# Forming spectral matrices in the first stage, loading layer 1's weights early, and moving the last image's put-back beside the long scan

## The chip, the cores and the metric

The kernel runs on one core of one Trainium2 chip. A core has five engines that matter here: TensorE (PE in the profile), VectorE (DVE), ScalarE (ACT), GpSimd (POOL) and SyncE (SP), which in this kernel does nothing but issue every DMA, in program order. The metric is the time of the whole program on the device, in microseconds (us). All arithmetic is in 32-bit floating point.

## What is computed

The input is four images of 128 channels and 64 x 64 pixels, 4096 tokens each. Two layers follow one another; cut to what matters:

```
# layer 0, per image
score  = gated two-convolution score of every 4x4 patch        # orders the 256 patches
x1n    = layernorm(x_reordered + pe)
xz     = x1n @ in_proj.T                                       # then conv1d, silu, dt, B, C
h      = dA_t * h + dB_t * x_t         # 16 states, 256 channels, 4096 steps
out_m  = (ys + D * xc) * silu(z) @ out_proj.T
x      = x + put_back(out_m)           # patches return to their places in the image

# layer 1, tokens of every image
state  = exp(delta A) * state + delta B x                      # 256 states, 256 channels
y      = state . C                     # then * silu(z) @ W_out, added to the tokens
t      = t + y
t      = t + sum over 4 branches of weight_i *
             ( sum_k conv(phi_k, t) @ (sigma_k**0.25 * M_plus[i, k])  # first 1/1, 1/2, 1/4, 1/8
             + the same with M_minus on sign-alternated tokens + a 3-tap term with M_u[i] )
```

The four branches act on the first 4096, 2048, 1024 and 512 tokens. Since they differ only in where they stop, their matrices can be added up beforehand: for every filter k and every range of tokens there is one summed matrix for M_plus and one for M_minus, and from these the sum P and the difference Q that the kernel multiplies with. These are the "spectral matrices". They depend on weights alone.

## The kernel before

The program is four stages in a row, each of which is a Python function that emits instructions.

`layer0_front` handles one image after another: statistics of the image, two 3 x 3 depthwise convolutions (four taps on TensorE, five on VectorE as `scalar_tensor_tensor` into the tile `sum`, line 105), Gelu on ScalarE (lines 187 and 209), the patch scores, the order of the patches as a permutation matrix (`perm_t`), and the ordered tokens (`xn`, written to DRAM as `xnt`). The order of instructions in this stage is chosen by the framework's own scheduler.

`layer0_scan` is scheduled by hand. It walks through 32 units of 512 tokens with a scan of 16 states on VectorE (line 506), and hides the projection of the next unit and the output of the last one beside it. Its function `put_back` takes the finished tokens of an image (`om`), multiplies them with `perm_t` on TensorE, adds the image (`xs`, line 440) and writes `x2`. For the last image this comes after the last scan.

`spectral_weights` loads M_plus and M_minus for each of the 16 filters (`raw`), sums the branches in `branch_sums` (a chain of `scalar_tensor_tensor` on VectorE), multiplies with sigma and writes P and Q to DRAM (`pqd`), and the summed M_u (`mud`).

`layer1` is scheduled by hand as well. It loads its weights, projects the first 512 tokens, and then runs 8192 steps: 32 parts (image, 512 tokens) of 256 states. One step of the loop `for k in range(-8, steps)` issues, for different states ahead of the current one:

- `fetch` (line 1084): a DMA that spreads two rows of delta over all partitions (`dlb`, four buffers), 8 steps ahead;
- `carry` (lines 1092 and 1093): two GpSimd instructions for 32 states that bring the last state of the part before into the first column, 6 steps ahead, in 28 of the 32 parts;
- `spread` (line 1098): the GpSimd product `v` for two states (three buffers), 4 steps ahead, and a small ScalarE copy (line 1102) that fills in the first column;
- `lift` (line 1107): two exponentials on ScalarE into `da`, which lies in PSUM in two buffers, 1 step ahead;
- `scan` (line 1110): the scan of one state on VectorE into `s`.

Every eight steps `contract` multiplies `s` with C on TensorE, copies the result with ScalarE into `ye` (one buffer, line 1133), writes it to DRAM (`yd`) and reads it back turned (`yt`). `beside` is a generator that hides two kinds of work in small pieces: `output` of the part before and `project` of the part after. A piece that says "free" moves one step, a piece that says "mm" or "post" moves at the seventh and eighth of each eight steps. Both call `normalise`, in which GpSimd forms `rs` and `ms` (lines 772 and 773) and ScalarE then uses them (line 777). `products` is a second generator: the convolutions of the spectral filters (`conv`, line 1058) and the products with P and Q (`fin`, line 1002) on TensorE, with `load` fetching `pq` (five buffers) and `strip` two items ahead. It goes by a credit per step, and what is left when the steps are over forms the tail.

Of the kernel before, what the change touches and what calls it, by code (L numbers as in the profile page):

```python
# [15 lines left out]
NB = 4  # L16
# [4 lines left out]


@with_exitstack
def layer0_front(ctx: ExitStack, tc, ident, half, w, x, xnt, perm_t):

# [84 lines left out]
    def by_patch(t, oy):  # L110

        return t.rearrange("c (py px oy ox) -> c oy py px ox", px=16, oy=4, ox=4)[:, oy]

    for b in range(NB):

        xs = xp.tile([128, L], F32, tag="xs", name="xs")
        nc.sync.dma_start(xs, x[b])
        st = sm.tile([128, 8, 6], F32, tag="st", name="st")
        for q in range(8):
            nc.vector.bn_stats(st[:, q, :], xs[:, bass.ts(q, 512)])  # L120
# [157 lines left out]


@with_exitstack  # L280
def layer0_scan(ctx: ExitStack, tc, ident, w, x, xnt, perm_t, x2):

# [250 lines left out]
    def gated(j):  # L533
        n, i, g = place(j)
        if i == 0:
            ygs[n] = big.tile([128, 2, PJ], F32, tag="yg", name="yg")
        cols = bass.ts(i, SUB)
        nc.vector.tensor_tensor(ygs[n][:, :, cols], y.pop((n, i)), ready[n][0][:, 2:4, cols], ALU.mult)
        if i == PJ // SUB - 1:
            b, unit = units[n]  # L540
            if unit == 0:
                oms[b] = big.tile([128, 2, 16, 128], F32, tag="om", name="om")
            behind.append(output(b, unit, ygs.pop(n), oms[b]))
            if unit == L // PJ - 1:
                behind.append(put_back(b, oms[b]))

    class Work:
        def __init__(self, pieces):
# [54 lines left out]
    gated(steps - 1)  # L603
    while holder or rear and rear.kind or behind:
        beside(steps)


TS = 512
# [4 lines left out]
NK = 16  # L613


@with_exitstack
def spectral_weights(ctx: ExitStack, tc, sigma, m_u, m_plus, m_minus, log_w, gumbel, pqd, mud):
# [39 lines left out]
    nc.vector.memset(quarter, 0.25)  # L657
    nc.gpsimd.tensor_tensor(sig, sig, quarter, ALU.pow)

    def branch_sums(dst, src):  # L660

        nc.vector.tensor_scalar(dst[:, 3], src[:, 0], wt[:, 0:1], None, ALU.mult)
        for i in range(1, 4):
            nc.vector.scalar_tensor_tensor(
                dst[:, 3 - i], src[:, i], wt[:, i : i + 1], dst[:, 4 - i], ALU.mult, ALU.add
            )

    mu = mp.tile([128, 4, 3, 128], F32, name="mu", bufs=1)
# [3 lines left out]
    branch_sums(mue, mu)  # L672
    nc.sync.dma_start(mud, mue)
    for k in range(NK):
        raw = mp.tile([128, 2, 4, 128], F32, tag="raw", name="raw")
        nc.sync.dma_start(raw[:, 0], m_plus[:, k].rearrange("i d e -> d i e"))
        nc.sync.dma_start(raw[:, 1], m_minus[:, k].rearrange("i d e -> d i e"))
        sums = mp.tile([128, 2, 4, 128], F32, tag="sums", name="sums")
        for side in range(2):
            branch_sums(sums[:, side], raw[:, side])  # L680
        nc.vector.tensor_scalar(sums, sums, sig[:, k : k + 1], None, ALU.mult)
        pq = mp.tile([128, 2, 4, 128], F32, tag="pq", name="pq")
        nc.vector.tensor_tensor(pq[:, 0], sums[:, 0], sums[:, 1], ALU.add)
        nc.vector.tensor_tensor(pq[:, 1], sums[:, 0], sums[:, 1], ALU.subtract)
        for side in range(2):
            nc.sync.dma_start(pqd[k, side], pq[:, side])


@with_exitstack
def layer1(ctx: ExitStack, tc, ident, half, w_in, w_delta, w_b, w_c, w_out, a_t, phi, pqd, mud, x2, x3, out):  # L690

# [27 lines left out]
    win = wp.tile([128, 512], F32, name="win")  # L719
    nc.sync.dma_start(win, w_in)  # L720
    wbd = wp.tile([128, 2, 512], F32, name="wbd")
    wc = wp.tile([128, 2, 256], F32, name="wc")
    for t, s in ((wbd[:, :, 0:256], w_b), (wbd[:, :, 256:512], w_delta), (wc, w_c)):
        nc.sync.dma_start(t, s.rearrange("(k p) n -> p k n", p=128))
    wo = wp.tile([128, 2, 128], F32, name="wo")
    nc.sync.dma_start(wo, w_out.rearrange("(k p) n -> p k n", p=128))
    at = wp.tile([128, 2, 256], F32, name="at")
    nc.sync.dma_start(at, a_t.rearrange("(k p) d -> p k d", p=128))
# [28 lines left out]
    def normalise(t):  # L757
# [13 lines left out]
        rs = sm.tile([128, NT], F32, tag="rs", name="rs")  # L771
        nc.gpsimd.tensor_tensor(rs, ve, half[:, :NT], ALU.pow)
        nc.gpsimd.tensor_tensor(ms, ms, rs, ALU.mult)
        yield "free"
        yield "free"
        for i in range(NT):
            nc.scalar.activation(  # L777
                t[:, i, :], t[:, i, :], AF.Identity, bias=ms[:, i : i + 1], scale=rs[:, i : i + 1]
# [12 lines left out]
    def project(b, ch, into):  # L791
# [73 lines left out]
                nc.vector.tensor_tensor(af[:, h, bass.ts(j, 128)], ps[:, 0:128], at[:, h, bass.ts(j, 128)], ALU.mult)  # L865
        yield "free"
        nc.scalar.activation(af, af, AF.Exp)

    tokens = {}

# [90 lines left out]
    def load(i):  # L961
# [125 lines left out]
    def carry(ch, d, ready):  # L1087

        af, vf = ready[4:]
        cols = bass.ds(d, 32)  # L1090
        if ch:
            nc.gpsimd.tensor_tensor(af[:, :, cols], af[:, :, cols], last[:, :, cols], ALU.mult)
            nc.gpsimd.tensor_tensor(vf[:, :, cols], vf[:, :, cols], af[:, :, cols], ALU.add)
# [21 lines left out]
    def contract(s, c, g, keep):  # L1115
# [13 lines left out]
                    )  # L1129

        def put(j):
            ye = wk.tile([128, 2, 32, GD], F32, tag="ye", name="ye", bufs=1)
            nc.scalar.copy(ye, yp[j].rearrange("p i d t -> p i t d"))  # L1133
            nc.sync.dma_start(yd[0:128, 2 * j : 2 * j + 2], ye)

# [56 lines left out]
    for k in range(-8, steps):  # L1192
# [62 lines left out]
def conv_attn_hybrid(ctx: ExitStack, tc, w, out):  # L1255
# [9 lines left out]
    x = w["x"]  # L1265
    with tc.tile_pool(name="ordered", bufs=1) as pool:
        xnt = dram.tile([NB, 128, 3 + L], F32, name="xnt")
        perm_t = pool.tile([128, NB, 2, 256], F32, name="perm_t")
        layer0_front(tc, ident, half, w, x, xnt, perm_t)
        layer0_scan(tc, ident, w, x, xnt, perm_t, x2)  # L1270
    pqd = dram.tile([NK, 2, 128, 4, 128], F32, name="pqd")
    mud = dram.tile([128, 4, 3, 128], F32, name="mud")
    spectral_weights(
        tc, w["sigma"], w["M_u"], w["M_phi_plus"], w["M_phi_minus"], w["log_weights"], w["gumbel"], pqd, mud
    )
    layer1(
        tc, ident, half, w["W_in"], w["W_delta"], w["W_B"], w["W_C"], w["W_out"], w["A"], w["phi"], pqd, mud,
        x2, x3, out,
    )


# ---- launch: one core; the host only lays the inputs out
# [45 lines left out]
```

## Time and profile before

| | us |
|---|---|
| time, median of 3 runs | 21922.89 |
| lowest and highest run | 21910.68, 21937.1 |
| span of the profiled execution | 21920.9 |
| busy, DVE | 20589.4 (94%) |
| busy, POOL | 20181.2 (92%) |
| busy, PE | 17505.8 (80%) |
| busy, ACT | 15831.5 (72%) |

The stages can be told apart in the timeline. The first stage ends with the last write of `xnt` at 569 us. The 16-state scan lasts from 642 us to 2753 us; the put-back of the last image follows until 2798 us, the spectral matrices until 2880 us, and the start of layer 1 until the first scan of 256 states at 2940 us. The 8192 steps last until 21566 us, and the tail until 21921 us. So a share of the whole span is an average over stages of which one, the 256-state loop, is 85%. Busy time counts an engine's own instructions; a row of the page gives how often a kind of instruction ran, the mean length of one, and the idle time of the engine just ahead of it.

### The profile page before, as it was taken

The numbers are of one execution on the slowest core, as the hardware profiler recorded it, in microseconds if no ns is written. First come the engines' busy times: TensorE is split into PE (matmuls) and PEld (weight loads), VectorE is DVE, ScalarE is ACT, GpSimd is POOL, SyncE is SP. The second block draws the span as 40 slices with busy tenths as digits, with TensorE's granted clock in tenths as the row PEclk, the third lists the DMA queues.
The fourth block names the chain that finished last, engine by engine and source line by source line (L and its number), as shares of the span: only waits on it lengthen the run. The fifth ranks groups of instructions, "written<-read, shape, count | busy, mean of one in ns | idle before, by whom it ended". The sixth has DMA issues, their size and how long they took to land.

```text
span 21920.9 us, 291965 instructions
## 1 busy us (share of the span) xinstructions
PE 17505.8 (80%) x98516; PEld 7675.8 (35%) x98516; DVE 20589.4 (94%) x11984; ACT 15831.5 (72%) x29148; POOL 20181.2 (92%) x5932
## 2 busy tenths in 40 slices
PE   7788844565858888877768888869498899999999
PEld 4344311232323333333323333324143344334344
DVE  6788979999999999999999999999999999999993
ACT  3677757777777777777777777777777777777773
POOL 0677769999999999999999999999999999999993
PEclk8999966676979999988979999979699999999999
DMA  0455544555756776666656777757477777777775
GB/s 31 123 139 140 140 143 150 168 181 159 215 171 217 219 222 216 219 206 193 200 185 215 221 218 219 220 180 228 154 232 217 225 232 233 231 231 230 229 227 152
DMA packets 2399968, 4238.08 MB, mean 193 GB/s; under 512 B 778200, under 2 KB 1235968, under 8 KB 2395136
## 3 DMA queue, kind: packets, MB, share of 16 engines
q1 hardware_dynamic: 2398464, 4219.40, 62.8%
q8 instruction: 776, 12.71, 0.2%
q14 instruction: 728, 5.96, 0.1%
HBM read 3600.52 MB, written 617.88 MB: 192 GB/s over the span
## 4 chain that ended last, share of the span: by engine, by line
DVE 50%; POOL 17%; PE 11%; ACT 9%; issue 7%; DMA 3%; SPq 0%; DVEq 0%; POOLq 0%; ACTq 0%
DVE s L1110 43%; POOL v L1098 17%; ACT da L1107 6%; PE conv L1058 5%; DVE states L506 3%; DMA yd<-ye 2%; PE yp L1127 2%; DVE p L510 1%; PE fin L1002 1%; ACT f L498 1%; PE y L522 1%; PE mm L415 1%; ACT t L777 0%; ACT ye L1133 0%; ACT xz L362 0%
## 5 line engine op out<-in xcount | busy, mean ns | idle before, releaser
L1098 POOL TENSOR_TENSOR v<-u,dlb 128x2044 f32<-128x2044 f32 x4096 | 18342.6, 4524 | 108.9 <-DMA dlb<-delta 89.9
L1110 DVE TENSOR_TENSOR_SCAN s<-da,v 128x1024 f32<-128x1024 f32 x8192 | 18055.4, 2269 | 384.0 <-ACT da L1107 309.2
L1107 ACT ACTIVATE da<-dlb,at 128x511 f32<-128x511 f32 x16384 | 11299.4, 690 | 2064.5 <-DVE s L1110 1599.6
L1058 PE MATMUL conv<-strip,tok 128*128 128x512 f32 (+3 forms) x20480 | 8653.9, 552 | 6.7 <-DMA strip<-in_phi 6.6
L1127 PE MATMUL yp<-s,c 128*32 128x256 f32 x65536 | 5011.0, 437 | 2958.7 <-DVE s L1110 1611.9
L1058 PEld LDWEIGHTS conv<-strip,tok 128*128 128x128 f32 x20480 | 3696.9, 193 | 4126.2 <-issue 3743.4
L1127 PEld LDWEIGHTS yp<-s,c 128*32 128x32 f32 x65536 | 1990.3, 121 | 6745.9 <-issue 1835.0
L1102 ACT COPY v<-vf 128x4 f32<-128x4 f32 x4096 | 813.3, 199 | 2262.8 <-DVE s L1110 2139.2
L484 POOL TENSOR_TENSOR v<-dx,bcb 128x1024 f32<-128x1024 f32 x512 | 1207.3, 2358 | 434.5 <-DVE states L506 427.6
L1002 PE MATMUL fin<-conved,pq 128*128 128x512 f32 (+1 forms) x3200 | 1423.6, 540 | 13.2 <-ACT conved L1069 4.4
L506 DVE TENSOR_TENSOR_SCAN states<-f,v 128x1024 f32<-128x1024 f32 x512 | 1175.9, 2297 | 173.1 <-ACT f L498 124.3
L1133 ACT COPY ye<-yp 128x512 f32<-128x512 f32 x2048 | 1185.9, 579 | 136.2 <-DMA yd<-ye 123.4
L498 ACT ACTIVATE f<-dt,an 128x255 f32<-128x255 f32 x2048 | 973.5, 476 | 419.0 <-DVE states L506 368.2
L522 PE MATMUL y<-p,ident 128*128 128x512 f32 x2048 | 1008.7, 622 | 147.3 <-DVE p L510 142.2
L1069 ACT COPY conved<-conv 128x512 f32<-128x512 f32 x1344 | 778.1, 579 | 340.4 <-PE conv L1058 339.4
L510 DVE TENSOR_TENSOR p<-states,bcb 128x1024 f32<-128x1024 f32 x512 | 627.0, 1225 | 39.3 <-DVE states L506 0.9
L1002 PEld LDWEIGHTS fin<-conved,pq 128*128 128x128 f32 x3200 | 533.3, 195 | 227.1 <-issue 165.8
L522 PEld LDWEIGHTS y<-p,ident 128*128 128x128 f32 x2048 | 370.2, 196 | 680.5 <-issue 355.7
L415 PE MATMUL mm<-ow,yg 128*32 128x128 f32 x2048 | 282.1, 297 | 106.8 <-ACT om L419 105.3
L415 PEld LDWEIGHTS mm<-ow,yg 128*32 128x32 f32 x2048 | 236.2, 139 | 213.0 <-ACT om L419 128.4
L136 POOL TENSOR_TENSOR rs<-sq,half 128x1 f32<-128x1 f32 x4 | 2.2, 559 | 329.6 <-DVE sq L134 329.6
L1018 DVE TENSOR_TENSOR xo<-xo,fin 128x512 f32<-128x512 f32 x32 | 21.3, 667 | 300.8 <-PE fin L1010 300.8
(239 smaller groups left out, 6143.4 us busy)
## 6 DMA issues: line engine op xcount, KB each, us to landing
dlb<-delta SPq DMA_DIRECT2D x4096, 512.0 KB, 4.1
strip<-in_phi SPq DMA_DIRECT2D x1536, 448.0 KB, 4.8
yd<-ye SPq DMA_DIRECT2D x2048, 256.0 KB, 4.0
bcb<-bcd SPq DMA_DIRECT2D x1024, 256.0 KB, 4.2
strip<-in_phi SPq DMA_DIRECT2D x1024, 256.0 KB, 4.3
pq<-pqd SPq DMA_DIRECT2D x1088, 64.0 KB, 3.9
yt<-yd SPq DMA_DIRECT2D x4096, 4.0 KB, 3.4
pq<-pqd SPq DMA_DIRECT2D x256, 128.0 KB, 4.1
```

Of the source, the lines that this page charges most:

```text
L484: nc.gpsimd.tensor_tensor(v, ready[n][2][:, :, bass.ts(i, SUB)].unsqueeze(1).broadcast_to((128, 2, 2, SUB)), bc[:, 0].unsqueeze(2).broadca ...
L498: nc.scalar.activation(factors[j % 2][:, a, k, 1:], ready[n][1][:, k, SUB * i + 1 : SUB * i + SUB], AF.Exp, scale=an[:, k, 2 * g + a : 2 * ...
L506: nc.vector.tensor_tensor_scan(states.rearrange(flat), factors[j % 2].rearrange(flat), v.rearrange(flat), 0.0, ALU.mult, ALU.add)
L510: nc.vector.tensor_tensor(p, states, bc[:, 1].unsqueeze(2).broadcast_to((128, 2, 2, SUB)), ALU.mult)
L522: nc.tensor.matmul(t.rearrange("p k t -> p (k t)"), ident, p[:, a].rearrange("p k t -> p (k t)"), start=g == 0 and a == 0, stop=False, ski ...
L1002: nc.tensor.matmul(fin[:, bass.ds(c0, w)], pq[:, n, :], u[:, bass.ds(c0, w)], start=begin and n == 0, stop=end and not partly, skip_group_ ...
L1058: nc.tensor.matmul(ps[:, skip:], tok[:, 1 - r if side else r, j, :], strip[:, bass.ds(c0 - lo, TS - skip)], start=src == sources[0] and j ...
L1098: nc.gpsimd.tensor_tensor(v[:, :, :, 1:], ready[0][:, :, 1:].unsqueeze(1).broadcast_to((128, VD, 2, TS - 1)), dl[:, :, 1:].unsqueeze(2).br ...
L1107: nc.scalar.activation(da[:, h, 1:], dl[:, d % VD, 1:], AF.Exp, scale=at[:, h, d : d + 1])
L1110: nc.vector.tensor_tensor_scan(s[:, d % GD].rearrange("p h t -> p (h t)"), da.rearrange("p h t -> p (h t)"), v[:, d % VD].rearrange("p h t ...
L1127: nc.tensor.matmul(yp[i // 2][bass.ts(q, 32), i % 2], c[:, h, t], s[:, :, h, t], start=h == 0, stop=h == 1)
L1133: nc.scalar.copy(ye, yp[j].rearrange("p i d t -> p i t d"))
```

## The change

Five things are done in one edit.

1. `spectral_weights` becomes a generator that `layer0_front` calls: a few filters at a time are emitted from the second image on, and the framework's scheduler places the instructions. The work moves to other engines: `branch_sums` scales on ScalarE (four copies of 256 values per filter, with weight times sigma in `both`) and adds on GpSimd (three additions of 256 values per filter, on both sides at once), and P and Q (512 values each) are formed on GpSimd.
2. `layer1_weights` loads the weights of layer 1 between the first two stages, into tiles that live as long as the program.
3. The put-back of the last image leaves `layer0_scan`. Its tokens and its permutation go to DRAM (`omd`, `permd`), and a new `put_back` in `layer1` does it in eight pieces beside the first part, in the place where the other parts have `output`.
4. `carry` takes 128 states at a time, 10 steps ahead.
5. `ye` gets two buffers, `pq` four in place of five, and `normalise` waits three steps more between GpSimd and ScalarE.

```
-def layer0_front(ctx: ExitStack, tc, ident, half, w, x, xnt, perm_t):
+def layer0_front(ctx: ExitStack, tc, ident, half, w, x, xnt, perm_t, pqd, mud):
...
+    matrices = spectral_weights(
+        ctx, tc, w["sigma"], w["M_u"], w["M_phi_plus"], w["M_phi_minus"], w["log_weights"], w["gumbel"], pqd, mud
+    )
     for b in range(NB):
...
         nc.sync.dma_start(xs, x[b])
+        for _ in range(6 if b else 0):
+            next(matrices, None)
...
             if unit == L // PJ - 1:
-                behind.append(put_back(b, oms[b]))
+                if b < NB - 1:
+                    behind.append(put_back(b, oms[b]))
...
+    for h in range(2):
+        nc.sync.dma_start(omd[h], oms[NB - 1][:, h])
...
-    def branch_sums(dst, src):
-
-        nc.vector.tensor_scalar(dst[:, 3], src[:, 0], wt[:, 0:1], None, ALU.mult)
+    both = cp.tile([128, 4, NK], F32, name="both")
+    for i in range(4):
+        nc.vector.tensor_scalar(both[:, i, :], sig, wt[:, i : i + 1], None, ALU.mult)
+
+    def branch_sums(dst, src, weight):
+
+        for i in range(4):
+            nc.scalar.activation(dst(3 - i), src(i), AF.Copy, scale=weight(i))
         for i in range(1, 4):
-            nc.vector.scalar_tensor_tensor(
-                dst[:, 3 - i], src[:, i], wt[:, i : i + 1], dst[:, 4 - i], ALU.mult, ALU.add
-            )
+            nc.gpsimd.tensor_tensor(dst(3 - i), dst(3 - i), dst(4 - i), ALU.add)
...
-        for side in range(2):
-            branch_sums(sums[:, side], raw[:, side])
-        nc.vector.tensor_scalar(sums, sums, sig[:, k : k + 1], None, ALU.mult)
+        branch_sums(lambda r: sums[:, :, r], lambda i: raw[:, :, i], lambda i: both[:, i, k : k + 1])
...
-        nc.vector.tensor_tensor(pq[:, 0], sums[:, 0], sums[:, 1], ALU.add)
-        nc.vector.tensor_tensor(pq[:, 1], sums[:, 0], sums[:, 1], ALU.subtract)
+        nc.gpsimd.tensor_tensor(pq[:, 0], sums[:, 0], sums[:, 1], ALU.add)
+        nc.gpsimd.tensor_tensor(pq[:, 1], sums[:, 0], sums[:, 1], ALU.subtract)
...
-        yield "free"
-        yield "free"
+        for _ in range(5):
+            yield "free"
...
+    def put_back():
+
+        b = NB - 1
+        image = lambda t, h, oy: t[b].rearrange("c (y oy x) -> c y oy x", oy=4, x=64)[:, bass.ts(h, 8), oy, :]
+        for h in range(2):
+            for oy in range(4):
+                om = wide().rearrange("p r (i c) -> p r i c", i=4)
+                for r in range(2):
+                    nc.sync.dma_start(om[:, r], omd[r][:, bass.ts(oy, 4)])
+                perm = sm.tile([128, 2, 128], F32, tag="mu", name="perm", bufs=1)
+                nc.sync.dma_start(perm, permd[:, :, bass.ts(h, 128)])
+                xs = small().rearrange("c (py x) -> c py x", x=64)
+                nc.sync.dma_start(xs, image(x, h, oy))
+                yield "mm"
+                ps = middle()
+                for ox in range(4):
+                    for r in range(2):
+                        nc.tensor.matmul(
+                            ps[:, bass.ts(ox, 128)], om[:, r, ox, :], perm[:, r, :], start=r == 0, stop=r == 1
+                        )
+                yield "post"
+                dst = xs.rearrange("c py (px ox) -> c py px ox", ox=4)
+                nc.vector.tensor_tensor(
+                    dst, dst, ps.rearrange("c (ox py px) -> c py px ox", ox=4, px=16), ALU.add
+                )
+                nc.sync.dma_start(image(x2, h, oy), xs)
...
-            pq = sp.tile([128, 2, 128], F32, tag="pq", name="pq", bufs=5)
+            pq = sp.tile([128, 2, 128], F32, tag="pq", name="pq", bufs=4)
...
-        cols = bass.ds(d, 32)
+        cols = bass.ds(d, 128)
...
-            ye = wk.tile([128, 2, 32, GD], F32, tag="ye", name="ye", bufs=1)
+            ye = wk.tile([128, 2, 32, GD], F32, tag="ye", name="ye")
...
             yield from output(*parts[n - 1], done.pop(n - 1), ready.pop(n - 1)[2])
+        else:
+            yield from put_back()
...
-        j = k + 6
-        if 0 <= j < steps and j % 32 == 0:
+        j = k + 10
+        if 0 <= j < steps and j % 128 == 0:
...
+        weights = layer1_weights(nc, const, *(w[k] for k in ("W_in", "W_delta", "W_B", "W_C", "W_out", "A")))
+        omd = dram.tile([2, 128, 16, 128], F32, name="omd")
+        permd = dram.tile([128, 2, 256], F32, name="permd")
+        nc.sync.dma_start(permd, perm_t[:, NB - 1])
```

More of the change, by code (lines that the diff above doesn't have):

```diff
@@ L280, in layer0_scan @@
 @with_exitstack
-def layer0_scan(ctx: ExitStack, tc, ident, w, x, xnt, perm_t, x2):
+def layer0_scan(ctx: ExitStack, tc, ident, w, x, xnt, perm_t, x2, omd):
     nc = tc.nc
@@ L613, with spectral_weights @@
 NK = 16
-@with_exitstack
-def spectral_weights(ctx: ExitStack, tc, sigma, m_u, m_plus, m_minus, log_w, gumbel, pqd, mud):
+def spectral_weights(ctx, tc, sigma, m_u, m_plus, m_minus, log_w, gumbel, pqd, mud):
     nc = tc.nc
@@ L671, in spectral_weights @@
     mue = mp.tile([128, 4, 3, 128], F32, name="mue", bufs=1)
-    branch_sums(mue, mu)
+    branch_sums(lambda r: mue[:, r], lambda i: mu[:, i], lambda i: wt[:, i : i + 1])
     nc.sync.dma_start(mud, mue)
+    yield
     for k in range(NK):
@@ L678, in spectral_weights, with layer1_weights, layer1 @@
         sums = mp.tile([128, 2, 4, 128], F32, tag="sums", name="sums")
-        for side in range(2):
-            branch_sums(sums[:, side], raw[:, side])
-        nc.vector.tensor_scalar(sums, sums, sig[:, k : k + 1], None, ALU.mult)
+        branch_sums(lambda r: sums[:, :, r], lambda i: raw[:, :, i], lambda i: both[:, i, k : k + 1])
         pq = mp.tile([128, 2, 4, 128], F32, tag="pq", name="pq")
-        nc.vector.tensor_tensor(pq[:, 0], sums[:, 0], sums[:, 1], ALU.add)
-        nc.vector.tensor_tensor(pq[:, 1], sums[:, 0], sums[:, 1], ALU.subtract)
+        nc.gpsimd.tensor_tensor(pq[:, 0], sums[:, 0], sums[:, 1], ALU.add)
+        nc.gpsimd.tensor_tensor(pq[:, 1], sums[:, 0], sums[:, 1], ALU.subtract)
         for side in range(2):
             nc.sync.dma_start(pqd[k, side], pq[:, side])
+        yield
+def layer1_weights(nc, pool, w_in, w_delta, w_b, w_c, w_out, a_t):
+    win = pool.tile([128, 512], F32, name="win")
+    nc.sync.dma_start(win, w_in)
+    wbd = pool.tile([128, 2, 512], F32, name="wbd")
+    wc = pool.tile([128, 2, 256], F32, name="wc")
+    for t, s in ((wbd[:, :, 0:256], w_b), (wbd[:, :, 256:512], w_delta), (wc, w_c)):
+        nc.sync.dma_start(t, s.rearrange("(k p) n -> p k n", p=128))
+    wo = pool.tile([128, 2, 128], F32, name="wo")
+    nc.sync.dma_start(wo, w_out.rearrange("(k p) n -> p k n", p=128))
+    at = pool.tile([128, 2, 256], F32, name="at")
+    nc.sync.dma_start(at, a_t.rearrange("(k p) d -> p k d", p=128))
+    return win, wbd, wc, wo, at
 @with_exitstack
-def layer1(ctx: ExitStack, tc, ident, half, w_in, w_delta, w_b, w_c, w_out, a_t, phi, pqd, mud, x2, x3, out):
+def layer1(ctx: ExitStack, tc, ident, half, weights, phi, pqd, mud, x, omd, permd, x2, x3, out):
     nc = tc.nc
@@ L717, in layer1 @@
     pf = ctx.enter_context(tc.tile_pool(name="s_pf", bufs=1, space=PSUM))
[L719 to L728, printed above, removed]
+    win, wbd, wc, wo, at = weights
     ones = wp.tile([128, 128], F32, name="ones")
@@ L1190, in fetch_y @@
                 take(done[m])
-    for k in range(-8, steps):
+    for k in range(-10, steps):
         now[0] = k
@@ L1267, in conv_attn_hybrid @@
         xnt = dram.tile([NB, 128, 3 + L], F32, name="xnt")
+        pqd = dram.tile([NK, 2, 128, 4, 128], F32, name="pqd")
+        mud = dram.tile([128, 4, 3, 128], F32, name="mud")
         perm_t = pool.tile([128, NB, 2, 256], F32, name="perm_t")
[L1269 to L1279, printed above, removed]
+        layer0_front(tc, ident, half, w, x, xnt, perm_t, pqd, mud)
+        weights = layer1_weights(nc, const, *(w[k] for k in ("W_in", "W_delta", "W_B", "W_C", "W_out", "A")))
+        omd = dram.tile([2, 128, 16, 128], F32, name="omd")
+        permd = dram.tile([128, 2, 256], F32, name="permd")
+        nc.sync.dma_start(permd, perm_t[:, NB - 1])
+        layer0_scan(tc, ident, w, x, xnt, perm_t, x2, omd)
+    layer1(tc, ident, half, weights, w["phi"], pqd, mud, x, omd, permd, x2, x3, out)
 def laid_out(inputs):
```

## Prediction

> **What bounds the kernel now.** I read the page first. Its rows name two engines that are nearly always busy in the 256-state loop:
>
> ```profile
> L1098 POOL TENSOR_TENSOR v<-u,dlb 128x2044 f32<-128x2044 f32 x4096 | 18342.6, 4524 | 108.9 <-DMA dlb<-delta 89.9
> L1110 DVE TENSOR_TENSOR_SCAN s<-da,v 128x1024 f32<-128x1024 f32 x8192 | 18055.4, 2269 | 384.0 <-ACT da L1107 309.2
> ```
>
> The chain of waits gives the scan 43% and `v` only 17%, which would point at VectorE. The groups of GpSimd between 2936 and 21566 us say otherwise:
>
> ```profile
> L1092 POOL TENSOR_TENSOR af<-af,last 128x64 f32<-128x64 f32 x224 | 74.2, 331 | 0.0
> L1093 POOL TENSOR_TENSOR vf<-vf,af 128x64 f32<-128x64 f32 x224 | 71.5, 319 | 17.5
> L772 POOL TENSOR_TENSOR rs<-ve,half 128x4 f32<-128x4 f32 x62 | 63.4, 1023 | 0.0
> L773 POOL TENSOR_TENSOR ms<-ms,rs 128x4 f32<-128x4 f32 x62 | 12.5, 202 | 4.9
> ```
>
> With `v` that is 18564 us busy, in a loop that for GpSimd lasts from 2935.7 to 21561.1 us, 18625 us: 61 us idle. The groups of VectorE in the same stretch sum to 18303 us, some 320 us idle. Two windows, the first two parts, show the same; the fifth pair of numbers is POOL:
>
> ```profile
> 2940.00:3514.00 574.00, 242.59 (x2028) 95.35 (x2028) 567.06 (x270) 413.40 (x756) 573.58 (x134) 0.61 0.46 149
> 3514.00:4094.00 580.00, 266.68 (x2124) 106.06 (x2128) 570.19 (x284) 420.10 (x775) 579.22 (x150) 0.61 0.47 151
> ```
>
> The first part, without `carry`, is 6 us shorter than the second, and GpSimd is full in both. So GpSimd bounds the loop, and ScalarE's delays are mostly absorbed by the three buffers of `v`. The waits of ScalarE and GpSimd there:
>
> ```profile
> ACT ye L1133 <- DMA yd<-ye: 121.2, 91, 5.8
> ACT t L777 <- POOL ms L773: 117.4, 56, 3.2
> ...
> POOL v L1098 <- DMA dlb<-delta: 89.9, 19, 42.8
> POOL v L1098 <- DVE s L1110: 15.9, 16, 5.2
> ```
>
> ScalarE loses over 230 us (and 114.6 us more to line 1093), but GpSimd loses only 15.9 us to VectorE, and 89.9 - 42.8 = 47 us to `dlb` (42.8 us is the start). Last the timeline at the seam, where nothing overlaps:
>
> ```profile
> 2763.91 0.58 ACT L419 COPY om<-mm 32x512 f32<-32x512 f32 x1 [2.05 <-PE mm L415]
> ...
> 2796.90 0.69 DVE L440 TENSOR_TENSOR xs<-xs,mm 128x512 f32<-128x512 f32 x1 [2.15 <-PE mm L434]
> ...
> 2883.20 0.47 SPq L796 DMA_DIRECT2D t<-x  x1
> 2888.01 0.72 PEld L800 LDWEIGHTS mm<-ident,t 128*128 128x128 f32 x4 [91.34 <-issue]
> ```
>
> The last `om` is done at 2764.5 us, and layer 1's first tokens are asked for 118.7 us later.
>
> [...]
>
> **Part one, the matrices in the first stage: +50 us.** Removed from the seam are their DVE instructions and DMAs (counted there). In the changed kernel's instruction order all 16 filters stand among the first image's work, from the third Gelu of line 187 (75 us) on: on POOL in one block between that image's `r` and the next image's `rs` (161.6 us before), on ACT in groups of 1 to 13 copies between the Gelus, which therefore wait behind copies that wait for POOL. POOL's price per value comes from the rows of lines 1092 and 1093 (64 values, 0.325 us) and from this line of the 16-state scan:
>
> ```profile
> 616.72 2.34 POOL L391 TENSOR_TENSOR e<-e,e 128x1024 f32<-128x1024 f32 x1 [150.95 <-DMA bcb<-bcd]
> ```
>
> That is 0.0021 us per value: 0.73 us for 256, 1.27 us for 512, 1.0 us for 384. 48 x 0.73 + 32 x 1.27 + 3 x 1.0 = 79 us. DVE has 52 convolution steps with two SBUF inputs left in that image (line 105, 0.67 us each: 35 us). The last Gelu is queued behind a copy that needs filter 13 finished, two filters (9.5 us) ahead of the end. Lower end, no contention: 78 + 79 - 9.5 = 147, some 5 us for `raw` loads that SP issues behind writes of `pqd`, so Gelu at about 153 instead of 129.5: +24. If POOL and DVE exclude each other: 78 + 79 + 35 - 9.5 = 182: +52. I take +50[...]; range +20 to +60. ACT's 64 copies and 4 of `mu` at about 0.5 us (33 us) lie inside this. The new small DVE instructions (some 20 of 0.2 us) mostly fill a wait for PE. On SP 16 loads stand ahead of the second image, but that load waits until 28.7 us anyway and is first read at 64.9 us. Images two to four are unchanged.
>
> **Part two, the seam: -113 us.** The put-back (33 us), the matrices (83 us) and the six weight loads (2.9 us of SP) go. In their place `omd`'s second half must land before the tokens may be asked for (in the changed kernel that load waits for both writes): 1 MB stores and loads of `xs` take 5.5 us to land (median). 118.7 - 5.7 = 113. Then the 52 us from line 800 to the first scan are as before[...]. The early weight loads lie beside the first stage. Range -118 to -100.
>
> **Part three, `carry`: -71 us.** 448 instructions of 64 values (145.7 us, and 17.5 us idle between the two) become 112 of 256 (112 x 0.73 = 82 us, and a quarter of the gaps, 4.4). Saved are 64 us by busy time, 77 with the gaps; I take 71. It is on GpSimd, the bound, so it counts fully. Issuing it earlier, the second `ye` and the longer wait in `normalise` end most of ScalarE's 353 us of waits; that buys only the 15.9 us above: -16 (0 to -45, if late `dlb` is also helped). VectorE then has 18309 us of work in some 18550.
>
> **Part four, `put_back` in the first part: +12 us.** Eight pieces: 64 matmuls on an idle PE and eight DVE additions (0.69 us) hide in their engines' slack. SP is the issue: each piece has a store that waits for the addition (as line 931 does, 86.9 us in 31 times, 2.8 each) and four loads, some 5 us of issue and waiting, ahead of the next `dlb`, which GpSimd needs. My estimate is that a `dlb` may be 5 to 8 us late. Five pieces stay within it; in three, SP also issues eight `yt` loads (5 us), and these cost about 4 us each. Range 0 to 48 (6 each). `pq` with four buffers waits for a `fin` matmul that stands one after the `conv` that `strip` waits for already: nothing, at most 1 us of SP per item. The tail is the same TensorE work.
>
> **Sum**, against the profiled span: 21920.9 + 50 - 113 - 71 - 16 + 12 = 21783; the runs' median is 2 us above that span, so 21785 us.
>
> **Rivals.** (a) No contention in the first stage: 21785 - 26 = 21759; for it, ScalarE's waits may space the additions out[...]. (b) Late `dlb`s: put-back costs 48, the front 60, and nothing comes of the -16: 21785 + 36 + 10 + 16 = 21847. (c) The loop was bound by ScalarE's stalls after all, so that removing them also frees the 47 us of `dlb` waits: 21740; against it, GpSimd's 61 us idle cap it. (d) Slower: `pq`'s new wait. SP holds every DMA; 10 tasks of the loop have one source per item, 640 items, and if each holds SP until PE reaches `fin`, `dlb` comes late. To end above 21965 it must cost GpSimd 180 us, 0.28 us per item. Each holds SP 1 us at most, but SP's time is only lost if `dlb`'s slack is used up; at 0.5 us each the time is 22105. Against it: `strip` waits for PE 559 times already (771 us on SP) and GpSimd loses 47 us to all DMAs. (e) The matrices don't hide: the front grows by their full 113 us; 21848, in (b)'s range.
>
> **How the numbers follow.** Forecast 0.5, (a) 0.14, (b) with (e) 0.2, (c) 0.1, (d) 0.06. 0.2% is 44 us, about what a measurement of this kernel can tell. Only (d) ends slower, 0.05, and its weak form falls within; same 0.04; faster 0.91. The range leaves out (d) and the ends of (b) and (c): 21715 to 21855.
>
> **What would show it.** Right: the first image's last write of `xnt` some 50 us later than 161.4 and the others keeping 135 us each, DVE's line 105 stretched beyond 0.67 us while GpSimd adds; 5 to 6 us between the last `om` and the tokens; 112 carry instructions of 0.73 us; GpSimd idle under 80 us in the loop, ScalarE's waits for `yd` and `ms` gone. Wrong: parts after the first longer than 581 us, or GpSimd waiting for `dlb` in every part.

## Result, and the profile after the change

The changed kernel takes 21745.58 us (median of 4 runs, 21742.0 to 21747.86), the kernel before 21924.06 us beside it (4 runs, 21910.68 to 21937.1). The ratio is 0.9918, with a 95% interval of 0.9901 to 0.9936: 178 us faster. The forecast was 21785 us; the time lies inside its range, 39 us below the forecast. The profiled span is 21744.9 us, 176.0 us less than before.

I cut both spans at the same places, the starts of the first and last scan of each kind. The loop is the stretch in which the 256-state steps run, the seam the stretch between the two scans, and the tail what follows the last scan:

| stretch | before | after | difference |
|---|---|---|---|
| start to first scan of 16 states | 642.3 | 681.0 | +38.7 |
| 16-state scan | 2104.4 | 2104.0 | -0.4 |
| its last scan to the first of 256 states (seam) | 193.6 | 78.2 | -115.4 |
| first to last scan of 256 states (loop) | 18623.1 | 18511.2 | -111.9 |
| tail | 357.5 | 370.5 | +13.0 |

So the gain comes from the seam and the loop in equal parts, and two stretches got longer. In the seam the timeline now shows this:

```profile
2802.26 0.58 ACT L426 COPY om<-mm 32x512 f32<-32x512 f32 x1 [2.05 <-PE mm L422]
2802.86 0.34 SPq L615 DMA_DIRECT2D omd<-om  x1
2806.92 0.32 SPq L814 DMA_DIRECT2D t<-x  x1
```

The tokens are asked for 4.1 us after the last `om` is done; before it was 118.7 us. In the loop the page's two rows of `v` and the scan, and the groups of GpSimd in that stretch, answer to those of before:

```profile
L1143 POOL TENSOR_TENSOR v<-u,dlb 128x2044 f32<-128x2044 f32 x4096 | 18333.8, 4536 | 68.1 <-DMA dlb<-delta 64.9
L1155 DVE TENSOR_TENSOR_SCAN s<-da,v 128x1024 f32<-128x1024 f32 x8192 | 18130.6, 2272 | 192.7 <-ACT da L1152 91.1
```

```profile
L790 POOL TENSOR_TENSOR rs<-ve,half 128x4 f32<-128x4 f32 x62 | 63.7, 1028 | 0.0
L1137 POOL TENSOR_TENSOR af<-af,last 128x256 f32<-128x256 f32 x56 | 42.2, 754 | 0.0
L1138 POOL TENSOR_TENSOR vf<-vf,af 128x256 f32<-128x256 f32 x56 | 40.6, 726 | 4.4
L791 POOL TENSOR_TENSOR ms<-ms,rs 128x4 f32<-128x4 f32 x62 | 12.5, 202 | 4.9
```

The two `carry` lines have 112 instructions in place of 448 and 82.8 us in place of 145.7. The first number after the bar is busy time, the last the idle time just ahead: 17.5 us between the two lines of `carry` has become 4.4. VectorE's idle time ahead of the scan was halved. GpSimd still is full in every part; the first two parts, with POOL again the fifth pair:

```profile
2863.20:3438.70 575.50, 270.84 (x2156) 121.79 (x2156) 571.16 (x278) 413.65 (x756) 574.32 (x133) 0.61 0.52 165
3438.70:4015.90 577.20, 264.85 (x2120) 104.78 (x2120) 572.46 (x283) 419.64 (x773) 576.88 (x138) 0.60 0.47 151
```

GpSimd's waits from 2950 to 21350 us (total, times, longest) are now:

```profile
POOL v L1143 <- DMA dlb<-delta: 20.9, 9, 3.5
POOL v L1143 <- DVE s L1155: 2.9, 1, 2.9
```

In the same window of the kernel before these were 47.1 and 15.9 us. ScalarE's waits for `ms` (117.4 us there) and for `yd` ahead of `ye` (121.2 us) are gone.

I also measured from the start of one `v` to the start of the next. The usual distance is 4.476 us, and what lies above it is what GpSimd lost. Where `carry` lies between two `v`, the loss was 154.1 us and is 84.2; where `rs` and `ms` do, 78.0 and 78.5; where nothing lies between, 59.6 and 17.1. The differences are -69.9, +0.5 and -42.5, and together they make up the loop's -111.9.

One reading of the prediction has to be set right here. Its 61 us of idle time on GpSimd come from adding up the busy time of rows that overlap one another a little. The idle times of its own lines give 108.9 - 42.8 + 17.5 + 4.9 = 88.5 us, and with overlaps counted once GpSimd is busy for 18536.9 us of the 18625.4. After the change it idles 33.3 us.

### The profile page after: what moved, and what is told of

Same layout as the page of the kernel before. It is cut to its first block, busy times and chain, and to the rows that moved or that the text cites. A ratio compares the mean times of both kernels' runs of the same rounds, so it can differ in the third digit from the quotient of the medians.

```text
span 21744.9 us, 291339 instructions
## 1 busy us (share of the span) xinstructions
PE 17469.3 (80%) x98516; PEld 7646.0 (35%) x98516; DVE 20628.6 (95%) x11808; ACT 15865.3 (73%) x29216; POOL 20221.1 (93%) x5679
## 4 chain that ended last, share of the span: by engine, by line
DVE 51%; POOL 23%; PE 9%; ACT 8%; issue 6%; DMA 2%; SPq 0%; DVEq 0%; POOLq 0%; ACTq 0%
DVE s L1155 44%; POOL v L1143 22%; ACT da L1152 5%; PE conv L1103 4%; DVE states L513 3%; DVE p L517 1%; PE yp L1172 1%; ACT f L505 1%; PE fin L1047 1%; PE y L529 1%; DMA dlb<-delta 1%; PE mm L422 1%; DMA yd<-ye 1%; PE conv L104 0%; DVE sum L106 0%
## 5 line engine op out<-in xcount | busy, mean ns | idle before, releaser
L517 DVE TENSOR_TENSOR p<-states,bcb 128x1024 f32<-128x1024 f32 x512 | 627.0, 1225 | 38.2 <-PE y L535 0.4
L356 PE MATMUL mm<-xin,taps 128*128 128x512 f32 x512 | 237.2, 606 | 28.3 <-DVE f L335 14.0
```

Source lines behind the costliest of these rows:

```text
L517: nc.vector.tensor_tensor(p, states, bc[:, 1].unsqueeze(2).broadcast_to((128, 2, 2, SUB)), ALU.mult)
```

## The experiments

Each kernel is set against the changed one unless said otherwise. The changed kernel and experiments 4, 5 and 7 have the same code in the loop, and their loops took 18511.2, 18518.7, 18514.6 and 18518.3 us, so differences under some 8 us in one trace are not read.

**1. The wait in `normalise` back to two steps.**

```
-        for _ in range(5):
+        for _ in range(2):
             yield "free"
```

> The changed kernel with two waiting steps in place of five in normalise. Theory (each part's output feeds the convolution queue eight steps later, the queue is dry at that moment, and the 14 matmuls that are missed land in the tail): the tail after the last scan falls from 370.5 to about 358 us, with 766 conv matmul records in it instead of 788; the loop loses some us, since ScalarE waits about 115 us for ms again and GpSimd's idle time rises from 17 towards 30 us. Total 21733 to 21750. Rival (the longer tail comes from four pq buffers or from the clock): the tail stays at 370 and the total rises by what the loop loses.

Measured: 21794.39 us, ratio to the kernel before 0.9938 (0.9923 to 0.9953), 49 us slower than the changed kernel. I had this wrong in total: I took the wait for a small matter. The trace splits it into a loop longer by 57.6 us and a tail shorter by 10.7 us. The waits in the loop's window, of ScalarE and then of GpSimd:

```profile
ACT t L795 <- POOL ms L791: 128.6, 57, 3.1
```

```profile
POOL v L1143 <- DMA dlb<-delta: 52.7, 22, 6.6
POOL v L1143 <- DVE s L1155: 14.5, 16, 4.9
```

ScalarE's wait for `ms` is back, and with it both of GpSimd's waits, at about the size of before. So of the small edits it is this one that took the idle time out of GpSimd. Most of GpSimd's larger stalls stand at one place, `v` number 36 of the 128 in a part: 54.1 of 74.7 us of stalls, in 19 of the 32 parts. There SyncE issues the store of the finished tokens, a load and eight reads of `yt` ahead of the next `dlb`. These transfers are in the changed kernel too, eight steps later (`v` number 40), where the stalls come to 22.3 us in 8 parts. SyncE does issue in step with ScalarE: 3563 of the 4096 loads of `dlb` waited in this window until ScalarE had made a `da` from an earlier one:

```profile
SPq L1129 <- ACT da L1152: 8142.8, 3563, 5.1
```

I read it so: a ScalarE that is 2.26 us later at each `ms` makes SyncE later against GpSimd, and the same block of DMAs then costs more. That the edit costs this time is shown; this path from ScalarE to `dlb` is my reading of the timeline.

**2. One buffer of `ye`.**

```
-            ye = wk.tile([128, 2, 32, GD], F32, tag="ye", name="ye")
+            ye = wk.tile([128, 2, 32, GD], F32, tag="ye", name="ye", bufs=1)
```

> The changed kernel with one ye buffer. Theory (late dlb loads came of ScalarE stalled by the write of ye, which holds back the release of dlb buffers): ScalarE waits about 120 us for the write again, GpSimd's idle time in the loop rises from 17 to about 45 us, total about +25 us. Rival (GpSimd never felt ScalarE's stalls): the waits of ScalarE return, GpSimd's idle time stays below 25 us, and the total is unchanged within 8 us.

Measured: 21757.73 us, ratio 0.9922 (0.9907 to 0.9936), 12 us slower; the loop is 18520.2 us. ScalarE's wait of `ye` for `yd` is back:

```profile
ACT ye L1178 <- DMA yd<-ye: 122.5, 87, 5.8
```

That is as much of ScalarE's time as the wait for `ms` (128.6 us in experiment 1), yet it costs at most 12 us where that one cost the loop 57.6. Here the sum of the waits of an engine that does not set the pace says nothing of their price.

**3. `carry` back to 32 states, 6 steps ahead.**

```
-        cols = bass.ds(d, 128)
+        cols = bass.ds(d, 32)
...
-        j = k + 10
-        if 0 <= j < steps and j % 128 == 0:
+        j = k + 6
+        if 0 <= j < steps and j % 32 == 0:
```

> The changed kernel with the carry as it was: 32 states at a time, 6 steps ahead. Theory (GpSimd is the bound, so its work counts fully): +70 us from 336 more instructions (154 against 84 us of extra time between two v), total about 21816. Rival (VectorE or ScalarE is the bound and GpSimd has room): under +20 us.

Measured: 21818.51 us, ratio 0.995 (0.9933 to 0.9966), 73 us slower; the loop is 18582.4 us, 71.2 longer. GpSimd's groups there:

```profile
L1143 POOL TENSOR_TENSOR v<-u,dlb 128x2044 f32<-128x2044 f32 x4095 | 18340.1, 4527 | 23.3 <-DMA dlb<-delta 23.2
L1137 POOL TENSOR_TENSOR af<-af,last 128x64 f32<-128x64 f32 x224 | 74.7, 333 | 0.0
L1138 POOL TENSOR_TENSOR vf<-vf,af 128x64 f32<-128x64 f32 x224 | 71.7, 320 | 17.5
```

The idle time ahead of `v` stays as small as in the changed kernel. So the width of `carry`, together with its earlier place, is worth its own length on GpSimd (with the gaps between its two instructions) and nothing else.

**4. The matrices between stages two and three, on VectorE, as before.** `spectral_weights` of before takes the place of the generator, with its call ahead of `layer1`.

```
-        for _ in range(6 if b else 0):
-            next(matrices, None)
...
+    spectral_weights(
+        tc, w["sigma"], w["M_u"], w["M_phi_plus"], w["M_phi_minus"], w["log_weights"], w["gumbel"], pqd, mud
+    )
```

> The changed kernel with the spectral matrices formed between the second and the third stage on VectorE, as before. Theory (moving them took away 83 us of a stretch where nothing else ran and gave back 39 us in the first image): first xnt back at 161 us, stretch before layer 1 longer by about 85 us, total about +44 us, 21790. Rival (the 39 us are the early weight loads or other edits): first xnt stays near 200 us.

Measured: 21798.63 us, ratio 0.994 (0.9925 to 0.9955), 53 us slower. The seam is 156.4 us, 78.2 longer; the start to the first scan is 642.8 us, 38.2 shorter. The rest of the 53 us (4 us in the 16-state scan, 7 in the loop) is within what such kernels differ by, so the move itself is worth some 40 us. The first `xnt` is written at 160.5 us again: what the first stage lost belongs to the matrices, not to the early weight loads. What those loads alone bring was not measured.

**5 and 6. The convolutions' sums in PSUM, in the changed kernel and in the one before.** The kernel keeps its tiles in two memories, SBUF and PSUM; its results of TensorE land in PSUM. The edit takes the second SBUF input away from VectorE's convolution steps. It also moves their result to PSUM, leaves two buffers in place of three, and lets the Gelus read PSUM. The kernel before with the same edit is the control for that.

```
-        sum_ = sm.tile([128, 8, 64], F32, tag="conv", name="sum", bufs=3)
+        sum_ = pq_.tile([128, 8, 64], F32, tag="conv", name="sum")
```

> The changed kernel with the tile sum of the convolutions in PSUM, two buffers in place of three in SBUF, so that VectorE's steps have one SBUF input. Read against the kernel before with the same edit. Theory (VectorE and GpSimd exclude each other while both read SBUF with two inputs): the first write of xnt comes about 24 us later than in the kernel before with the same edit, instead of 39; GpSimd's additions take 0.73 us again. Rival (only the order of ScalarE's queue delays the first image): still about 39 us later.

> The control: the kernel before with the tile sum in PSUM in two buffers. Both theories: the first stage changes[...]; nothing else changes.

Measured: 21750.07 us (ratio 0.9919, 0.9904 to 0.9934) and, for the control, 21943.67 us (ratio 1.0007, 0.9998 to 1.0016). Against this control the change is worth 193.6 us in place of 178.5, but both totals carry scatter, and the edit itself makes the later images slower (138.8 us each in place of 135.7). That isn't a price of PSUM per step: the steps with `f`, `w2b` and `sum` take 752 ns in the control and 750 before. Two buffers in place of three may be the reason; no run tells. The first image shows more. In the changed kernel, VectorE's groups by form from 60 to 210 us (busy, mean ns):

```profile
L106 DVE SCALAR_TENSOR_TENSOR sum<-f,w2b,sum 128x512 f32<-128x512 f32 x32 | 41.5, 1307 | 0.8
L106 DVE SCALAR_TENSOR_TENSOR sum<-xg,w,sum 128x512 f32<-128x512 f32 x32 | 33.6, 1103 | 0.1
L106 DVE SCALAR_TENSOR_TENSOR sum<-f,w2b,conv 128x512 f32<-128x512 f32 x8 | 5.9, 737 | 8.8 <-PE conv L104 5.8 <-ACT f L215 3.0
```

and GpSimd's in the same window:

```profile
L679 POOL TENSOR_TENSOR sums<-sums 128x256 f32<-128x256 f32 x48 | 47.5, 989 | 5.5 <-ACT sums L677 3.1
L696 POOL TENSOR_TENSOR pq<-sums 128x512 f32<-128x512 f32 x16 | 24.3, 1518 | 0.0
L695 POOL TENSOR_TENSOR pq<-sums 128x512 f32<-128x512 f32 x16 | 22.3, 1394 | 1.3
```

With the sums in PSUM the same groups of the two engines are:

```profile
L107 DVE SCALAR_TENSOR_TENSOR sum<-f,w2b,sum 128x512 f32<-128x512 f32 x32 | 23.0, 753 | 0.5
L107 DVE SCALAR_TENSOR_TENSOR sum<-xg,w,sum 128x512 f32<-128x512 f32 x32 | 21.6, 751 | 0.1
```

```profile
L680 POOL TENSOR_TENSOR sums<-sums 128x256 f32<-128x256 f32 x48 | 34.9, 727 | 11.4 <-ACT sums L678 8.9
L697 POOL TENSOR_TENSOR pq<-sums 128x512 f32<-128x512 f32 x16 | 20.5, 1282 | 0.0
L696 POOL TENSOR_TENSOR pq<-sums 128x512 f32<-128x512 f32 x16 | 20.3, 1269 | 1.3
```

Both engines stretch each other where VectorE has two inputs in SBUF: VectorE by 30 us (41.5 + 33.6 against 23.0 + 21.6), GpSimd by 18.4 us (94.1 against 75.7). The form whose second input is `conv`, in PSUM, keeps 737 ns even in the changed kernel, though it writes to SBUF like the others and runs beside GpSimd's additions. So it is the second SBUF input that counts: 1307 ns with it, 737 without. A stretch of the timeline of the changed kernel shows it pair by pair:

```profile
143.29 4.49 DVE L106 SCALAR_TENSOR_TENSOR sum<-f,w2b,sum 128x512 f32<-128x512 f32 x4
143.80 3.43 POOL L679 TENSOR_TENSOR sums<-sums 128x256 f32<-128x256 f32 x3
147.31 1.60 POOL L695 TENSOR_TENSOR pq<-sums 128x512 f32<-128x512 f32 x1
```

Four VectorE steps take 1.12 us each in place of 0.75, three additions 1.14 us each in place of 0.73. Their plain lengths add up to 5.2 us, and together they took 4.5: it is nearly as if the two took turns. And for the first image's last write of `xnt`, the first of the two start times in these rows, of the kernel before, of the changed kernel, of the one with the sums in PSUM and of the control:

```profile
L272 SPq DMA_DIRECT2D xnt<-xn x4: 326/327/330, 161.4 to 568.6; - x4
```

```profile
L278 SPq DMA_DIRECT2D xnt<-xn x4: 319/319/320, 200.7 to 607.5; - x4
```

```profile
L279 SPq DMA_DIRECT2D xnt<-xn x4: 319/320/320, 189.8 to 606.2; - x4
```

```profile
L273 SPq DMA_DIRECT2D xnt<-xn x4: 326/326/331, 165.2 to 581.7; - x4
```

Without contention the matrices delay the first image by 189.8 - 165.2 = 24.6 us, with it by 200.7 - 161.4 = 39.3 us. So 14.7 us is the contention. The start of the first 16-state scan says the same: 680.2 - 655.4 = 24.8 us without it, 38.7 with it. The other 24.6 us I put down to the Gelus, which queue behind ScalarE's copies; with the sums in PSUM these copies wait 35.3 us for `raw` and 6.2 us for GpSimd's `pq`. No run takes these two apart.

**7. The matrices of the filters beside the 16-state scan.** The setup and the summed M_u stay in the first stage; each filter's four copies and five additions are issued one at a time, over the steps of the 16-state scan, on the same engines. P and Q are written back into `raw`.

```
-        for _ in range(6 if b else 0):
-            next(matrices, None)
+        if b == 1:
+            next(matrices)
...
         beside(j)
+        next(matrices, None)
```

> The changed kernel with the 16 filters' matrices formed in small pieces beside the 16-state scan instead of in the first stage (the branch weights and the summed M_u stay there). Theory (the matrices cost only because VectorE and ScalarE are on the first image's path; in the 16-state scan VectorE bounds, its inputs come from PSUM, and GpSimd is idle 22%): first xnt back near 163 us, the 16-state scan not longer by more than 6 us, total about -37 us, 21709. Rival (GpSimd's or ScalarE's extra work holds up the scan): the scan grows by 30 us or more and nothing is won.

Measured: 21722.08 us, ratio 0.9907 (0.9892 to 0.9921), 23.5 us faster than the changed kernel. The whole of the first stage's 38 us comes back (first 16-state scan at 642.9 us), and the scan is hardly longer: 2106.6 us here and 2111.1 in experiment 9, which has the same edit, against 2100.6 to 2108.1 in the kernels without it. Its additions there have their plain length:

```profile
L702 POOL TENSOR_TENSOR raw<-sums 128x512 f32<-128x512 f32 x32 | 40.6, 1268 | 0.0
L698 POOL TENSOR_TENSOR sums<-sums 128x256 f32<-128x256 f32 x48 | 34.8, 726 | 0.0
```

Of the missing 14 us, the trace puts 7.1 in the loop and 2.6 in the scan. In the loop this kernel lies at the others' level and the changed kernel's own trace at their lower end. The rest doesn't show in the trace. That I can't separate from scatter.

**8. Three steps in `normalise`,** and **9. the same with the matrices beside the 16-state scan.**

```
-        for _ in range(5):
+        for _ in range(3):
             yield "free"
```

> The changed kernel with three steps of waiting in place of five between GpSimd's ms and ScalarE's use of it. With two steps ScalarE waited 2.26 us on average for ms, 57 times, and a step is 2.26 us long: one more step should take most of that wait away, and with it most of the 57.6 us that the loop lost. With three steps ScalarE's use falls on the sixth of the eight steps, still ahead of the place where the next matrix piece may go, so the output pieces should come eight steps earlier than with five and the tail should have 828 convolution records instead of 849. Theory: loop 18511 to 18526 us, tail 358 to 361 us, time 21735 to 21750 us. Rival one, the tail follows the length of the wait itself and not the place among the eight steps: tail 363 to 367 us. Rival two, the loop needs the shift by eight steps and not the shorter wait: loop about 18560 us, time about 21785 us.

> The changed kernel with the matrices of the 16 filters in small pieces beside the 16-state scan, and three steps of waiting in normalise. If the two edits add up, the time is that of the matrices beside the scan alone (21722) less what three steps bring in the tail (11 us) plus at most some us of stalls: 21711 to 21727 us, the best of all kernels here. If the shorter wait costs the loop its 57 us, 21770 us.

Measured: 21743.83 us (ratio 0.9916, 0.9902 to 0.9929) and 21708.96 us (ratio 0.99, 0.9886 to 0.9913). The tail of the first is 356.5 us, of the second 358.3. ScalarE's wait in the loop's window of the first:

```profile
ACT t L795 <- POOL ms L791: 21.0, 45, 0.7
```

One step more than two takes 107.6 of the 128.6 us away, and the loop is 18518.9 us, that of the others. So the loop needs the wait filled, not a shift by eight steps, and three steps fill it. TensorE's largest groups in the tail, of the changed kernel and then of this one:

```profile
L1103 PE MATMUL conv<-strip,tok 128*128 128x512 f32 (+3 forms) x790 | 274.6, 489 | 0.0
L1047 PE MATMUL fin<-conved,pq 128*128 128x512 f32 x200 | 103.2, 598 | 0.0
```

```profile
L1103 PE MATMUL conv<-strip,tok 128*128 128x512 f32 (+1 forms) x767 | 264.0, 486 | 0.0
L1047 PE MATMUL fin<-conved,pq 128*128 128x512 f32 x194 | 99.2, 594 | 0.0
```

With five steps ScalarE's use falls on the eighth of the eight steps, just past the place where the next matrix piece may go, so the output's remaining pieces come eight steps later; 23 matmuls of the convolutions and 6 of the products more are then left when the steps are over, and TensorE is busy for 359.5 of the tail's 370.5 us. With three steps it falls on the sixth, and the tail is that of before. Four or five buffers of `pq` make no difference to the tail (370.5 us, and 370.3 in experiment 11). In the time of the first kernel this shows as only 2 us, within the scatter; together with the matrices beside the scan it is 13 us (21722.1 to 21709.0), and that version is the fastest of all, 37 us below the changed kernel. The intervals of the two ratios still touch, since both carry the scatter of the kernel before; the runs themselves lie apart (21699.17 to 21712.76 against 21742.0 to 21747.86).

**10. The last image put back between the stages, as before.**

```
-                if b < NB - 1:
-                    behind.append(put_back(b, oms[b]))
+                behind.append(put_back(b, oms[b]))
...
-    for h in range(2):
-        nc.sync.dma_start(omd[h], oms[NB - 1][:, h])
...
-        else:
-            yield from put_back()
```

> The changed kernel with the last image put back between the 16-state scan and layer 1, as before. Theory: the put-back took 33 us there and the writes that replace it take 4.1 us, so the seam grows by 28 us, and the first part, which no longer holds the eight pieces, gains 1 to 2 us: time 21745.6 + 27 = 21772 us. The forecast had charged 12 us in the first part: then 21761 us. If the pieces had cost nothing and the loads at the start of layer 1 were hidden by the put-back as well: under 21757 us.

Measured: 21774.39 us, ratio 0.9931 (0.9917 to 0.9944), 28.8 us slower, and as the theory had it: the seam is 26.8 us longer and the first part 574.3 us in place of 575.5. In the other kernels that hold the eight pieces, the first part takes 574.4 to 577.0 us. So the pieces cost the loop 0 to 3 us, not 12.

**11. Five buffers of `pq` with one of `ye`,** set beside experiment 2.

```
-            pq = sp.tile([128, 2, 128], F32, tag="pq", name="pq", bufs=4)
+            pq = sp.tile([128, 2, 128], F32, tag="pq", name="pq", bufs=5)
```

> The changed kernel with one buffer of ye and five of pq, to be set beside the one with one buffer of ye and four of pq (21757.7 us). Theory: the wait of pq's load for the buffer falls with the wait of the strip load beside it and costs nothing: 21755 to 21760 us. Rival (d) in a weak form, SyncE loses time to that wait and dlb comes late: then five buffers take 10 us or more off, 21748 us or less.

Measured: 21756.72 us, ratio 0.9922 (0.9908 to 0.9935), 1 us from experiment 2. The wait is real; with four buffers SyncE's waits in the loop of experiment 2 list it, and with five it falls to 9.4 us:

```profile
SPq L1014 <- PE fin L1047: 205.8, 155, 4.4
```

But 206 us of SyncE's time cost the kernel nothing that can be measured: rival (d) is excluded.

## Why the prediction was right, and where its steps were off

The direction and the two large terms were right. In the order of its sum:

- **Matrices in the first stage: +50 forecast, +39 measured.** The mis-sized term is the contention: 26 us, from +24 to the +50 taken, charged as if GpSimd lost the length of nearly every VectorE step. That a VectorE step with two SBUF inputs and a GpSimd addition contend was my assumption, which the kernel before doesn't show, and it didn't settle how much is lost. It cost 14.7 us, because GpSimd lost only 18.4 us, while VectorE's steps took 30 us more, and part of that filled idle time (11.4 us ahead of its additions became 5.5). The lower end, +24 against the 24.6 of experiments 5 and 6, is closer than its working was: it priced the delay of the last Gelu, and that was 27.6 us there and 44.5 in the changed kernel (129.5 to 174.0 us); the stretch from this Gelu to the write of `xnt` then was 3 to 5 us shorter, which the prediction didn't foresee. ScalarE's 64 copies, which the prediction took at about 0.5 us each, took 496 ns. Rival (a), no contention, and the full 113 us of rival (e) are both excluded. Images two to four took 135.6 us each, as forecast.
- **Seam: -113 forecast, -115.4 measured.** The wait for `omd` was 4.1 us where 5.5 was taken. Experiment 10 gives the put-back's share, 27 us net in the seam, and experiment 4 that of the matrices, 78 us. The remaining 10 us, the early weight loads among them, no run takes apart.
- **`carry`: -71 forecast, -69.9 measured,** and 71 to 73 by experiment 3. Its instructions of 256 values took 754 and 726 ns against the 730 taken.
- **The other small edits: -16 forecast, about -44 measured** (-42.5 with the put-back's cost in it). This is the largest miss. The step that failed is "that buys only the 15.9 us above": it counted GpSimd's waits for VectorE, which fell to 2.9 us, but left `dlb`'s 47 us alone because the profile puts them down to a DMA. By my reading the DMA was late because SyncE issues in step with ScalarE. Rival (c) had this link from ScalarE to `dlb`; the 61 us that were to cap it were really 88.5. That its 21740 us came nearer than the forecast is partly luck: 20.9 of its 47 us stayed, and the 11 us that it overcharged in the first stage and the 13 us of tail that it left out nearly cancel. Experiment 1 names the edit, the wait in `normalise`; neither the second `ye` (at most 12 us) nor the early `carry` (experiment 3 keeps GpSimd's idle time low without it) does the work.
- **`put_back` in the first part: +12 forecast, 0 to 3 measured** (experiment 10). The late `dlb`s of that step, and of rival (b), did not come: the first part of the changed kernel has one stall of 1.0 us between two `v` and one of 0.1.
- **Tail: 0 forecast, +13 measured.** "The tail is the same TensorE work" overlooked that what the loop leaves undone depends on the step at which the last tokens are ready. Experiments 1 and 8 show that the longer wait moves it.
- **Total.** 39 - 115 - 70 - 42 + 13 = -175, against -138 in the forecast. The matrices miss by -11 us, the small edits with the put-back by -38, the seam and `carry` by 2 or less. The tail's +13 hid a part of this, which is luck.
- **The signs named.** Line 105 (now 106) stretched, to 1.31 and 1.10 us on average in the first image, against 0.74 to 0.75 us before and not the 0.67 that the prediction read off a stretch of overlapping steps. GpSimd's idle time below 80 us is no sign as it stands, since the prediction's own 61 us already were; by the gaps it fell from 88.5 to 33.3. `dlb` is waited for 9 times and not in every part. The sign of being wrong, parts longer than 581 us, did appear, weakly: 4 of the 31 distances between the starts of parts exceed it, by 0.7 at most, and the mean of those after the first is 578.7.
- **A detail of the reading.** The kernel before runs a pair of the kind that contends in one place: three VectorE steps of 384 values on `mue` (617 to 620 ns) beside a GpSimd instruction of 16 values (2.91 us). With nothing to compare it to, it shows no contention either way.

What stays open: with two steps of wait the changed kernel loses 74.9 us between two `v`, more than the 59.6 us of the kernel before, though its `ye` has two buffers. That the rarer pauses for `carry` leave SyncE less room to catch up would fit, but no run tells it apart. Nor does a run test the path from ScalarE's wait to the late `dlb` by itself.

## What to carry to other kernels

Ask of each wait on an engine that is not the bound what is queued behind it and who issues the bound engine's transfers: here 122 us of one ScalarE wait cost 12 us at most, and 129 us of another cost the loop 58. Before moving additions to GpSimd, look at what VectorE runs beside them; the same 80 additions with their copies cost 39 us beside the convolutions, 15 of them for the second SBUF input, and at most some 7 us beside a scan in which GpSimd idles 433.5 us ahead of its products. Where a schedule has fixed places, as here, a wait of three steps in place of two leaves the tail as it was, and one of five moves the work behind it by a whole period of eight steps.

## What was not expected of the hardware

The contention between VectorE and GpSimd is mutual: in the same stretch GpSimd's additions of 256 values went from 727 to 989 ns on average (1251 at most) and VectorE's steps of 512 from 750 to 1307. The prediction had treated the two as excluding each other with the whole loss on GpSimd. The trace shows instructions of both lengthened, by up to 524 ns for an addition (1251 against 727) and up to 1042 ns for a VectorE step (1794 against 752). The first is less than the length of one VectorE step; the second is more than one addition of 256 values takes, and less than one of 512 (1269).
